# A four-layer graph network on one core: layer 0's second product in Strassen's form, and the order of emission kept on four engines

## The chip, the core and the metric

The kernel runs on one core of one Trainium2 chip. A core has five engines that work at the same time, each from its own queue, in the order of that queue: TensorE (PE: matmuls, with a weight load PEld ahead of each), VectorE (DVE), ScalarE (ACT), GpSimd (POOL) and SyncE (SP, which here only issues DMAs). The metric is device time of one launch in microseconds (us); lower is better. The time before is 2439.52 us, the median of three runs (2439.32 to 2441.19).

## What is computed

Input x holds 128 graphs of 64 nodes with 256 features, in f32, with one 64x64 adjacency matrix for all. Four layers follow one another, each as `x = layernorm(x + layer(x))`. Layer 0 is the one that the change rewrites:

```python
A_norm = A + jnp.eye(n)
A_hat = A_norm * dinv[:, None] * dinv[None, :]
agg = jnp.einsum('nm,bmd->bnd', A_hat, features)
h = jax.nn.relu(_batchnorm(agg.reshape(-1, d) @ W1.T + b1, g1, be1))   # 512 wide
out = _batchnorm(h @ W2.T + b2, g2, be2)                               # 256 wide
```

Both batch norms take mean and variance over all 128 x 64 rows, so nothing behind one can begin before all rows in front of it are done. Layer 1 normalises a Laplacian by the largest eigenvalue of the adjacency matrix (`lam_max = eigvalsh(L)[-1]`), and has a dense layer, attention over the graph and a feed-forward part, with layer norms between. Layer 2 is two graph convolutions and four LSTMs over windows of 1 to 4 nodes, layer 3 one graph attention.

## The kernel before

**Blocks and buffers.** The 8192 rows are cut into 16 blocks of 512 rows. A block is a tile of 128 partitions x 1024 values, either with tokens or with features on the partitions. There are four PSUM tiles (`PS`) and eight SBUF scratch tiles (`mem`); both are handed out and given back by hand.

**Who sets the order.** Each piece of work is a generator. Before it emits instructions it yields `step(engine, us, ps, sl, ...)`: the engine (T is PE, V DVE, S ACT, G POOL, Q a DMA issue), a planned cost, and the PSUM and scratch tiles that it needs. `flow()` (L130) holds a clock for each engine, always lets the step begin that can begin soonest, and so emits the instructions of all generators in one interleaved order. A step that is ready is planned 2.0 us later on PE than it could begin (0.5 us on DVE and ACT in the second flow) unless its stream is `urgent`. There are two flows: one for layer 0 with the eigenvalue, and one for all the rest. After that, the framework's scheduler places the emitted instructions in each engine's queue, and may put a later one ahead of an earlier one. In the built program, counted by emission number, 392 of the 7236 matmuls and transposes on PE stand behind one that is emitted after them, and 1326 of the 2864 instructions on DVE.

**Layer 0.** `first_block` (L523): aggregation with the adjacency (L322, eight products of 128 columns), a copy out of PSUM (DVE L537), two halves of the first dense product (L346, four products of 512 columns each), each followed by two evictions with bias on ACT (L549) and two batch norm statistics on DVE (L553). `bn_coeffs` (L501): aggregates of the statistics (DVE L508), a power on POOL (L511), three small products and sums on DVE (L513 to L515). `second_block` (L556): four relus with the batch norm's scale and shift on ACT (L561), eight products of 512 columns with W2T (PE L566: two halves of output features, four chunks of input features), two evictions (ACT L575), two statistics (DVE L579).

**The eigenvalue**, `eig` (L446): 26 rounds. Each squares a 128x128 matrix M on PE (L468), takes its trace on DVE (L471, L473) and PE (a product with ones, L476), and scales M by one over the trace (DVE L479, L481). Its generator runs in the same stream as the blocks, so its rounds lie between their products. It holds one PSUM tile, `e_ps`, until the flow has ended. From the result it makes `LnT` (L499), the matrix with which layer 1 aggregates.

**From layer 0 to layer 1.** Between the flows the code emits weight loads and a few small instructions. W2 of layer 1 goes to `WB[:, 2:4]` (L609). `wL` and the LSTM biases `bih`, `bhh` (L855 to L872) are loaded into memory that layer 0's pool has given back, and DVE adds the two biases (L873). Then the second flow begins with `end_block` (L631: batch norm on ACT L638, transposes L340, residual sum on DVE L646, layer norm with statistics L272 to L274, the power on POOL L308, the application on ACT L314) and `block` (L652: layer 1; aggregation L322, copy L660, dense product L358, sum L669, a layer norm on DVE with L297 and L300, residual L673, transposes L334, projections L346).

**The LSTMs** (`lstm`, L922) have steps p > 1 in Strassen's form already: seven products of half the rows (L1024) with sums on DVE (L1068, L1070, L1083, L1090, L1092), one on POOL (L1072) and copies on ACT (L1064).

Of the kernel before, what the change touches and what calls it, by code (L numbers as in the profile page):

```python
# [10 lines left out]
AF = mybir.ActivationFunctionType  # L11
ALU = mybir.AluOpType
# [21 lines left out]
def kernel(ctx: ExitStack, tc: tile.TileContext, a: dict, out: bass.AP):  # L34
    nc = tc.nc
    V, S, G, T = nc.vector, nc.scalar, nc.gpsimd, nc.tensor

    def bc_mid(ap, n):

# [10 lines left out]
    def fm(s):  # L50

        return s.rearrange("p (c k) -> p c k", c=2)
# [159 lines left out]
    def ctile(shape, name, pool=cp):  # L212
        return pool.tile(shape, F32, tag=name, name=name)
# [152 lines left out]
    def by_chunk(ap):  # L366
        return ap.rearrange("(k p) m -> p k m", p=P)
# [19 lines left out]
    with c0:  # L387
# [7 lines left out]
        cols = {k: ctile([P, 4 if j < 3 else 2], f"l0{k}", wp) for j, k in enumerate(("b1", "g1", "be1", "b2", "g2", "be2"))}  # L395
        nc.scalar.dma_start(cols["b1"], a["L0_gnn_b1"])
        W2T = ctile([P, 4, D], "W2T", wp)

        def later_loads():
            for k in cols:  # L400
                if k != "b1":
                    yield step("Q", 1.0)
                    nc.sync.dma_start(cols[k], a[f"L0_gnn_{k}"])
            yield step("Q", 6.0)
            nc.sync.dma_start(W2T, by_chunk(a["L0_gnn_W2"]))
            yield step("V", 1.2)
            V.tensor_tensor(adj2, bdA[:, :N], bdA[:, N:], ALU.add)

            V.tensor_scalar(cap1, adj2, 0.0, BIG, ALU.is_gt, ALU.mult)
            V.tensor_scalar(cap1, cap1, -1.0e9, None, ALU.add)  # L410

            V.tensor_scalar(cap3, adj2, 0.0, 2.0, ALU.not_equal, ALU.mult)
            V.tensor_scalar(cap3, cap3, -1.0, BIG, ALU.add, ALU.mult)
# [8 lines left out]
        def etile(name, n=P, bufs=2):  # L422
            return ep.tile([P, n], F32, tag=name, name=name, bufs=bufs)
# [19 lines left out]

        def eig():  # L446
            yield step("V", 1.2)
            V.tensor_scalar(Sy, Sy, 0.5, None, ALU.mult)
# [13 lines left out]
            V.tensor_scalar(sh, sh, 1e-30, None, ALU.add)  # L462
            M = etile("eM")
            V.scalar_tensor_tensor(M, ident, sh, Sy, ALU.mult, ALU.add)
            for _ in range(EIG_STEPS):
                yield step("T", 0.5)
                pm = pse(P)
                T.matmul(pm, M, M, start=True, stop=True)  # L468
                yield step("V", 0.6)
                t_ = etile("etmp")  # L470
                V.tensor_tensor(t_, pm, ident, ALU.mult)  # L471
                d_ = etile("ed", 2)
                V.reduce_sum(d_[:, 0:1], t_, axis=AX.X)  # L473
# [23 lines left out]
            t_ = etile("etmp")  # L497
            V.tensor_scalar(t_, bdAT, 2.0, r_, ALU.mult, ALU.mult)
            V.tensor_tensor(LnT, t_, ident, ALU.subtract)  # L499

        def bn_coeffs(name, nch, st, g, be):  # L501

# [53 lines left out]
        def second_block(i):  # L556
            sc1, sh1 = bn["bn1"]
            src = [(fm(Xs[i]) if f < 2 else H[i])[:, f % 2, :] for f in range(4)]
            yield step("S", 2.8)
            for f in range(4):  # L560
                S.activation(src[f], src[f], AF.Relu, scale=sc1[:, f : f + 1], bias=sh1[:, f : f + 1])  # L561
            yield step("T", 6.9, ps=1)
            ps = PS.take()
            for c in range(2):
                for f in range(4):
                    T.matmul(  # L566
                        fm(PS[ps])[:, c, :],
                        W2T[:, f, c * P : (c + 1) * P],
                        src[f],
                        start=(f == 0),  # L570
                        stop=(f == 3),
                    )
            yield step("S", 1.3, ps=-1)
            for c in range(2):
                S.activation(H[i][:, c, :], fm(PS[ps])[:, c, :], AF.Identity, bias=cols["b2"][:, c : c + 1])  # L575
            PS.give(ps)
            yield step("V", 1.25)
            for c in range(2):
                V.bn_stats(st2[:, c, i, :], H[i][:, c, :])  # L579
            mark("l0b", i)  # L580

        blocks = range(NBLK)
        tasks = [(None, lambda i=i: first_block(i), 2) for i in blocks]
        tasks[1:1] = [(None, eig, 0)]
        tasks[4:4] = [(None, later_loads, 0)]
        tasks.append(
            (
                lambda: ready(*[("l0a", i) for i in blocks]),
# [1 line left out]
                0,  # L590
            )
        )
        tasks += [(lambda: ready(("bn1",)), lambda i=i: second_block(i), 0) for i in blocks]
        tasks.append(
            (
                lambda: ready(*[("l0b", i) for i in blocks]),
# [1 line left out]
                0,  # L598
            )
        )  # L600
        flow([Stream(6, 0, tasks)], {"T": 2.0})
        PS.give(0)


        Wc, Wq, Wk, Wv = (WA[:, j, :].rearrange("p (k m) -> p k m", k=2) for j in range(4))
# [1030 lines left out]
```

## Time and profile before

| | |
|---|---|
| median of 3 runs | 2439.52 us (2439.32 to 2441.19) |
| the profiled execution | 2439.17 us, of which the span from the first to the last instruction is 2437.4 us |
| PE busy | 2348.3 us, 96% of the span, mean granted clock 0.983 |
| DVE, ACT, POOL busy | 1215.1, 1169.9 and 566.7 us (50%, 48%, 23%) |
| DMA | 57.5 MB, 24 GB/s on average |

The profile comes from one execution. Its page has the busy time of each engine, the span in 40 slices, the chain that ended last, and groups of equal instructions with the idle time in front of them and who ended it. "PE L340 <- ACT h L964" reads: PE stood idle ahead of an instruction of line 340, and what released it was the instruction of line 964 on ACT that works on a tile h. A matmul in f32 appears as two records (two passes), a transpose as one. The granted clock is the rate of PE's clock, 1.00 or 0.50 at any one time in this trace; a stage's number is the mean over it.

### The profile page before, as it was taken

The page shows a single profiled execution, that of the slowest core. Times are in us where ns is not written, and L with a number is a line of the kernel's source. Part 1 is how long each engine was busy: PE and PEld are TensorE (multiplying, and loading weights), DVE is VectorE, ACT ScalarE, POOL GpSimd, SP SyncE. Part 2 cuts the span into 40 slices and gives each one's busy share as a digit, 9 for nine tenths or more (in the row PEclk, how much of TensorE's full clock was granted, in tenths as well). Part 3 has the DMA queues.
Part 4 walks back from the last instruction along what each step waited for, and adds up shares of the span by engine and source line. Part 5 has one row for each costly group of instructions (what it writes and reads, how often), then busy time and mean ns, then how long its engine had stood idle before and what let it go on. Part 6 is the DMA issues. An engine that isn't in the chain of part 4 may idle for free. (4 is left out here: it accounts for less than half of the span.)

```text
span 2437.4 us, 33965 instructions
## 1 busy us (share of the span) xinstructions
PE 2348.3 (96%) x13700; PEld 1798.9 (74%) x13700; DVE 1215.1 (50%) x2864; ACT 1169.9 (48%) x2138; POOL 566.7 (23%) x426
## 2 busy tenths in 40 slices
PE   8999889999999999999999999999999999998997
PEld 5544567766676666676676788899999888887785
DVE  4542377646475345744462433344435444455446
ACT  2255453543444444335544444444444654468766
POOL 0000034222333222422231221222212222122112
PEclk9999989999999999999999999999999999999998
DMA  5110111000000000000010000000001000001111
GB/s 172 44 52 0 40 31 49 27 9 10 1 10 18 10 9 10 1 10 34 20 61 1 18 1 1 1 18 1 1 1 35 1 9 10 18 27 66 40 35 44
DMA packets 40974, 57.47 MB, mean 24 GB/s; under 512 B 4592, under 2 KB 33904, under 8 KB 40816
## 3 DMA queue, kind: packets, MB, share of 16 engines
q1 hardware_dynamic: 39712, 54.22, 6.9%
q8 instruction: 107, 1.75, 0.3%
q10 hardware_dynamic: 1104, 1.08, 0.1%
q14 instruction: 51, 0.42, 0.1%
HBM read 38.52 MB, written 16.78 MB: 23 GB/s over the span
## 5 line engine op out<-in xcount | busy, mean ns | idle before, releaser
L1024 PE MATMUL ps<-x,x 128*128 128x256 f32 x1024 | 248.6, 380 | 0.7 <-DVE t L1092 0.7
L1024 PEld LDWEIGHTS ps<-x,x 128*128 128x128 f32 x1024 | 191.5, 190 | 26.4 <-issue 1.6
L314 ACT ACTIVATE x<-x,ln_nm,ln_rs 128x256 f32<-128x256 f32 x196 | 103.7, 592 | 97.0 <-DVE ln_nm L311 95.5
L1024 PE MATMUL ps<-t,x 128*128 128x256 f32 x576 | 141.0, 379 | 0.0
L308 POOL TENSOR_TENSOR ln_rs<-ln_rs,neghalf 128x4 f32<-128x4 f32 (+1 forms) x72 | 70.5, 980 | 231.1 <-DVE ln_rs L274 217.3
L1024 PEld LDWEIGHTS ps<-t,x 128*128 128x128 f32 x576 | 108.6, 190 | 14.6 <-issue 0.4
L346 PE MATMUL ps<-t,W1T 128*128 128x512 f32 x256 | 115.2, 593 | 0.0
L952 PE MATMUL ps<-h,wL 128*128 128x192 f32 (+2 forms) x504 | 111.6, 375 | 0.0
L952 PEld LDWEIGHTS ps<-h,wL 128*128 128x128 f32 x504 | 79.1, 190 | 27.6 <-issue 26.7
L272 DVE BATCH_NORM_STATS2 ln_st<-x 128x6 f32<-128x256 f32 x256 | 98.2, 404 | 0.5
L1100 ACT ACTIVATE t<-t,bih 128x512 f32<-128x512 f32 (+2 forms) x63 | 41.0, 652 | 107.6 <-DVE t L1090 105.9
L952 PE MATMUL ps<-h,x 128*128 128x256 f32 x384 | 86.8, 379 | 0.0
L964 ACT ACTIVATE t<-ps,bih 128x512 f32<-128x512 f32 (+3 forms) x104 | 61.5, 642 | 44.0 <-PE ps L952 43.9
L294 POOL TENSOR_TENSOR ln_rs<-ln_rs,neghalf 128x4 f32<-128x4 f32 x32 | 36.9, 1153 | 188.8 <-DVE ln_rs L274 188.6
L346 PEld LDWEIGHTS ps<-t,W1T 128*128 128x128 f32 x256 | 46.3, 190 | 46.4 <-issue 46.4
L952 PEld LDWEIGHTS ps<-h,x 128*128 128x128 f32 x384 | 72.9, 190 | 10.3 <-issue 0.5
L1083 DVE COPY t<-ps 128x256 f32<-128x256 f32 (+2 forms) x63 | 23.7, 378 | 113.5 <-PE ps L1024 113.5
L273 DVE BATCH_NORM_AGGREGATE ln_mv<-ln_st 128x2 f32<-128x6 f32 x448 | 71.3, 167 | 0.0
L346 PE MATMUL ps<-t,wA 128*128 128x512 f32 x144 | 67.9, 617 | 2.8 <-ACT t L681 2.8
L952 PE MATMUL ps<-t,wL 128*128 128x512 f32 x144 | 64.9, 607 | 2.5 <-ACT t L1250 2.5
L1090 DVE TENSOR_TENSOR t<-ps,t 128x512 f32<-128x512 f32 (+2 forms) x63 | 38.1, 604 | 54.8 <-PE ps L1024 47.9
L1100 ACT ACTIVATE x<-x,bih 128x512 f32<-128x512 f32 (+2 forms) x57 | 36.6, 641 | 55.7 <-DVE x L1090 55.4
(692 smaller groups left out, 5688.2 us busy)
## 6 DMA issues: line engine op xcount, KB each, us to landing
t<-in_x_dram SPq DMA_DIRECT2D x26, 512.0 KB, 3.9
xd<-x SPq DMA_DIRECT2D x16, 512.0 KB, 2.6
x<-xd SPq DMA_DIRECT2D x6, 512.0 KB, 3.3
out_dram<-x SPq DMA_DIRECT2D x6, 512.0 KB, 3.0
wL<-in_L_gnn_Wih_dram SPq DMA_DIRECT2D x2, 1024.0 KB, 4.9
h<-in_x_dram SPq DMA_DIRECT2D x4, 512.0 KB, 4.2
x<-in_L_gnn_Whh_dram SPq DMA_DIRECT2D x2, 1024.0 KB, 4.9
t<-xd SPq DMA_DIRECT2D x4, 512.0 KB, 3.3
```

Of the source, the lines that this page charges most:

```text
L272: V.bn_stats(st[:, t, :], y[:, t, :])
L273: V.bn_aggr(mv[:, t, :], st[:, t, :])
L294: G.tensor_tensor(rs, rs, neghalf[:, :NT], ALU.pow)
L308: G.tensor_tensor(rs, rs, neghalf[:, :n], ALU.pow)
L314: S.activation(y[:, t, :], y[:, t, :], AF.Identity, scale=rs[:, t : t + 1], bias=nm[:, t : t + 1])
L346: T.matmul(ps[:, c, :], w[:, k, (off + c) * P : (off + c + 1) * P], yT[:, k, :], start=(k == 0), stop=(k == nk - 1),)
L952: T.matmul(spread(fm(PS[ps])[:, j, :n], q), WL[p][0][:, k, m], x_of(0, q)[:, k], start=(k == 0), stop=(k == 1),)
L964: S.activation(of(sl)[:, j], fm(PS[ps])[:, j, :n], AF.Tanh if g == 2 else AF.Sigmoid, bias=bias(g, c))
L1024: T.matmul(dst, WS[p][name](k, g), y[:, k], start=first and k == 0, stop=k == 1, skip_group_check=not first)
L1083: V.tensor_copy(y[:, 1, :], v[:, 0, :])
L1090: V.tensor_tensor(y[:, 0:2, :], v[:, 2:4, :], y[:, 0:2, :], ALU.add)
L1100: S.activation(of(act[g])[:, 0], of(act[g])[:, 0], f, bias=bias(g, 0))
```

## The change

One: `manual_schedule` keeps the order of emission on PE, DVE, ACT and POOL. The order of SP's DMAs stays with the scheduler.

Two: `second_block` of block 0 runs by chunks (relu of chunk f, then both products with it); blocks 1 to 15 use Strassen's form, with rows split in halves u and v and features in halves x (chunks 0, 1) and h (chunks 2, 3). Seven products of 256 columns, each over two chunks, take the place of eight of 512. Four sums of weights are made once (into the place of layer 1's W2), and each block takes two of the scratch tiles for T1 to T4.

Three: in `eig` only every third round takes the trace and scales; the other squares are copied out of PSUM as they are (26 squares as before, 8 traces in place of 26). It moves to a stream of its own, ahead of the blocks and urgent, and gives its PSUM tile back when it is done.

Four: `later_loads` moves from fifth to fourth place in the tasks.

```diff
+    ctx.enter_context(tc.manual_schedule(engines={E.PE, E.DVE, E.Activation, E.Pool}))
...
+        W2S = WB[:, 2:4, :].rearrange("p a (b k m) -> p (a b) k m", b=2, k=2)
...
+            yield step("V", 1.7)
+            (a11, a21), (a12, a22) = ([W2T[:, k : k + 2, c * P : (c + 1) * P] for c in range(2)] for k in (0, 2))
+            V.tensor_tensor(W2S[0], a21, a22, ALU.add)
+            V.tensor_tensor(W2S[1], W2S[0], a11, ALU.subtract)
+            V.tensor_tensor(W2S[2], a11, a21, ALU.subtract)
+            V.tensor_tensor(W2S[3], a12, W2S[1], ALU.subtract)
...
-            for _ in range(EIG_STEPS):
+            for j in range(EIG_STEPS):
...
+                if j % 3 < 2:
+                    yield step("V", 0.35)
+                    M = etile("eM")
+                    V.tensor_copy(M, pm)
+                    continue
...
+            if i == 0:
+                for f in range(4):
+                    yield step("S", 0.7)
+                    relu(f)
+                    yield step("T", 1.75, ps=int(f == 0), waits=f == 3)
...
+            x, h = fm(Xs[i]), H[i]
+            u, v = slice(0, TB // 2), slice(TB // 2, TB)
+            yield step("V", 1.4, sl=2)
...
+            V.tensor_tensor(T1, x[:, :, v], x[:, :, u], ALU.subtract)
+            V.tensor_tensor(T2, h[:, :, v], T1, ALU.subtract)
+            yield step("G", 1.3, waits=False)
+            G.tensor_tensor(T4, h[:, :, u], T2, ALU.subtract)
+            yield step("V", 0.7)
+            V.tensor_tensor(T3, h[:, :, v], x[:, :, v], ALU.subtract)
...
+            product(A11, x[:, :, u], p[:, 0, :], first=True)
+            product(W2S[0], T1, p[:, 3, :], first=True)
+            yield step("S", 0.75, waits=False)
+            S.copy(y[:, 0, :], p[:, 0, :])
+            S.copy(y[:, 3, :], p[:, 3, :])
+            t = yield step("T", 1.75)
+            product(A12, h[:, :, u], p[:, 2, :])
+            product(W2S[3], h[:, :, v], p[:, 3, :])
+            yield step("T", 0.88)
+            product(W2S[1], T2, p[:, 0, :])
+            yield step("V", 0.42)
+            V.tensor_copy(y[:, 1, :], p[:, 0, :])
+            yield step("T", 0.88)
+            product(W2S[2], T3, p[:, 0, :])
+            yield step("V", 1.1)
+            V.tensor_tensor(y[:, 3, :], p[:, 0, :], y[:, 3, :], ALU.add)
+            V.tensor_tensor(y[:, 0:2, :], p[:, 2:4, :], y[:, 0:2, :], ALU.add)
+            yield step("T", 0.88)
+            product(A22, T4, p[:, 0, :])
...
+            yield step("S", 1.5, ps=-1)
+            S.activation(h[:, 0, :], fm(Xs[i])[:, 0, :], AF.Identity, bias=cols["b2"][:, 0:1])
+            S.activation(h[:, 1, v], y[:, 3, :], AF.Identity, bias=cols["b2"][:, 1:2])
+            S.activation(h[:, 1, u], p[:, 0, :], AF.Identity, bias=cols["b2"][:, 1:2])
...
-        tasks[1:1] = [(None, eig, 0)]
-        tasks[4:4] = [(None, later_loads, 0)]
+        tasks[3:3] = [(None, later_loads, 0)]
...
-        tasks += [(lambda: ready(("bn1",)), lambda i=i: second_block(i), 0) for i in blocks]
+        tasks += [(lambda: ready(("bn1",)), lambda i=i: second_block(i), 2) for i in blocks]
...
-        flow([Stream(6, 0, tasks)], {"T": 2.0})
-        PS.give(0)
+        flow([Stream(1, 0, [(None, eig, 0)], urgent=True), Stream(6, 1, tasks)], {"T": 2.0})
```

More of the change, by code (lines that the diff above doesn't have):

```diff
@@ L36 @@
     V, S, G, T = nc.vector, nc.scalar, nc.gpsimd, nc.tensor
+    E = mybir.EngineType
+    ctx.enter_context(tc.manual_schedule(engines={E.PE, E.DVE, E.Activation, E.Pool}))
     def bc_mid(ap, n):
@@ L397 @@
         W2T = ctile([P, 4, D], "W2T", wp)
+        W2S = WB[:, 2:4, :].rearrange("p a (b k m) -> p (a b) k m", b=2, k=2)
+        W2S = [W2S[:, j] for j in range(4)]
         def later_loads():
@@ L499, in eig @@
             V.tensor_tensor(LnT, t_, ident, ALU.subtract)
+            PS.give(0)
         def bn_coeffs(name, nch, st, g, be):
@@ L558, in second_block, with relu @@
             src = [(fm(Xs[i]) if f < 2 else H[i])[:, f % 2, :] for f in range(4)]
+            def relu(f):
+                S.activation(src[f], src[f], AF.Relu, scale=sc1[:, f : f + 1], bias=sh1[:, f : f + 1])
+            if i == 0:
[3 more added lines that the diff above has]
+                    yield step("T", 1.75, ps=int(f == 0), waits=f == 3)
+                    if f == 0:
+                        ps = PS.take()
+                    for c in range(2):
+                        T.matmul(
+                            fm(PS[ps])[:, c, :],
+                            W2T[:, f, c * P : (c + 1) * P],
+                            src[f],
+                            start=(f == 0),
+                            stop=(f == 3),
+                        )
+                yield step("S", 1.3, ps=-1)
+                for c in range(2):
+                    S.activation(H[i][:, c, :], fm(PS[ps])[:, c, :], AF.Identity, bias=cols["b2"][:, c : c + 1])
+                PS.give(ps)
+                yield from second_stats(i)
+                return
@@ L559, in second_block @@
             yield step("S", 2.8)
             for f in range(4):
-                S.activation(src[f], src[f], AF.Relu, scale=sc1[:, f : f + 1], bias=sh1[:, f : f + 1])
-            yield step("T", 6.9, ps=1)
-            ps = PS.take()
[L564 to L572, printed above, removed]
@@ L573, in second_block @@
-            yield step("S", 1.3, ps=-1)
-            for c in range(2):
-                S.activation(H[i][:, c, :], fm(PS[ps])[:, c, :], AF.Identity, bias=cols["b2"][:, c : c + 1])
+                relu(f)
+            x, h = fm(Xs[i]), H[i]
+            u, v = slice(0, TB // 2), slice(TB // 2, TB)
+            yield step("V", 1.4, sl=2)
+            slots = [mem.take() for _ in range(2)]
+            T1, T2, T3, T4 = (
+                mem[sl][:, j * TB : (j + 1) * TB].rearrange("p (c k) -> p c k", c=2) for sl in slots for j in range(2)
+            )
@@ new lines, in second_block, with product @@
+            V.tensor_tensor(T1, x[:, :, v], x[:, :, u], ALU.subtract)
[4 more added lines that the diff above has]
+            V.tensor_tensor(T3, h[:, :, v], x[:, :, v], ALU.subtract)
+            def product(w, y, dst, first=False):
+                for k in range(2):
+                    T.matmul(
+                        dst, w[:, k, :], y[:, k, :], start=first and k == 0, stop=k == 1, skip_group_check=not first
+                    )
@@ new lines, in second_block @@
+            A11, A12, A22 = (W2T[:, k : k + 2, c * P : (c + 1) * P] for k, c in ((0, 0), (2, 0), (2, 1)))
+            yield step("T", 1.75, ps=1)
+            ps = PS.take()
+            p, y = (m.rearrange("p (j k) -> p j k", j=4) for m in (PS[ps], Xs[i]))
+            product(A11, x[:, :, u], p[:, 0, :], first=True)
[3 more added lines that the diff above has]
+            S.copy(y[:, 3, :], p[:, 3, :])
@@ L576, in second_block @@
+            yield step("T", 0.88)
+            product(A22, T4, p[:, 0, :])
+            for sl in slots:
+                mem.give(sl)
+            yield step("S", 1.5, ps=-1)
+            S.activation(h[:, 0, :], fm(Xs[i])[:, 0, :], AF.Identity, bias=cols["b2"][:, 0:1])
+            S.activation(h[:, 1, v], y[:, 3, :], AF.Identity, bias=cols["b2"][:, 1:2])
+            S.activation(h[:, 1, u], p[:, 0, :], AF.Identity, bias=cols["b2"][:, 1:2])
             PS.give(ps)
+            yield from second_stats(i)
@@ L577, in second_block, with second_stats @@
+        def second_stats(i):
             yield step("V", 1.25)
```

## The prediction, made before the changed kernel ran

> **What bounds the kernel now.** I read the table of stages first: for each stretch its length, then the busy time of PE, PEld, DVE, ACT and POOL with the number of records, then PE's granted clock.
>
> ```profile
> 0.00:155.00 155.00, 147.83 (x578) 86.32 (x578) 78.69 (x160) 40.49 (x63) 2.50 (x15) 1.00 0.36 105
> 155.00:161.00 6.00, 1.94 (x10) 1.37 (x8) 4.12 (x14) 2.24 (x4) 1.01 (x1) 0.72 0.00 1
> 161.00:277.00 116.00, 115.60 (x291) 53.28 (x290) 28.60 (x66) 63.31 (x94) 0.00 (x0) 0.98 0.00 0
> 277.00:283.00 6.00, 1.33 (x5) 0.98 (x5) 4.84 (x20) 2.05 (x4) 0.70 (x1) 0.80 0.01 1
> 283.00:337.00 54.00, 39.48 (x288) 30.07 (x287) 41.27 (x126) 42.09 (x66) 19.23 (x17) 0.85 0.25 74
> 337.00:2180.00 1843.00, 1816.57 (x11096) 1443.54 (x11097) 919.70 (x1978) 826.09 (x1458) 491.97 (x326) 0.99 0.04 13
> 2180.00:2438.00 258.00, 225.55 (x1441) 183.39 (x1439) 137.91 (x505) 193.59 (x454) 51.31 (x66) 0.95 0.15 50
> ```
>
> PE is full in layer 0's products (rows 1 and 3) and nearly full from 337 to 2180: there only PE work that disappears, or a hole in PE, moves the end. The two batch norms (155, 277) and the start of layer 1 (283 to 337) are chains with PE waiting. Behind 337 PE stands idle 1843 - 1816.6 = 26 us, and 32 us behind 2180. A hole costs twice: the granted clock is below 1.00 after it.
>
> Second, the rows of ACT and PE around the largest hole behind 337 (start, length, engine, line, what, [idle before <- who ended it]):
>
> ```profile
> 516.92 1.09 ACT L314 ACTIVATE x<-x,ln_nm,ln_rs 128x256 f32<-128x256 f32 x2 [4.30 <-DVE ln_nm L311]
> 517.92 0.61 ACT L991 ACTIVATE t<-h 128x512 f32<-128x512 f32 x1
> 518.44 1.08 ACT L314 ACTIVATE x<-x,ln_nm,ln_rs 128x256 f32<-128x256 f32 x2
> 519.42 1.24 ACT L964 ACTIVATE h<-ps,bih 128x512 f32<-128x512 f32 x2
> ```
> ```profile
> 520.72 0.69 PE L340 MATMUL ps<-ident,h 128*128 128x128 f32 x2 [3.37 <-ACT h L964]
> ```
>
> PE waits 3.4 us for a PSUM tile that ACT (L964) has not emptied, since ACT stands before a layer norm (L314) that waits for DVE. By emission number L964 (2888) comes ahead of L314 (2932): the scheduler turned them round. The hole at 580 (3.5 us, also "ACT h L964") has the same form: L964 (3236) stands behind L991 (3258), which waits for POOL.
>
> **The change, part by part.** PE's order hardly moves (392 of 7236 out of emission order before); DVE's (1326 of 2864) and ACT's do.
>
> Strassen. In the last rows of the stage ACT empties one block's PSUM every 7.09 us:
>
> ```profile
> 269.38 1.26 ACT L575 ACTIVATE h<-ps,l0b 128x512 f32<-128x512 f32 x2 [5.83 <-PE ps L566]
> 276.47 1.26 ACT L575 ACTIVATE h<-ps,l0b 128x512 f32<-128x512 f32 x2 [5.83 <-PE ps L566]
> ```
>
> In between lie 16 records of L566, whose weight loads follow at 0.4285 us (13 steps from 262.69 to 268.26), so 6.86 us, and one of eig's products, so 0.23 us. Fourteen products of 256 columns are 28 records; the LSTMs' stretch 1400 to 1420 has 94 such in 20.0 us, 0.2128 each, so 5.96 us. 15 blocks x 0.90 = **-13.5**. Beside it, per block: on ACT four relus at 0.70 from start to start and five further instructions (L1064 0.37 twice, L575 0.68, L1104 0.45 twice), 5.1 us; on DVE three sums (L1070, 0.68), a copy and two sums (0.42, 0.41, 0.68) and two statistics (0.68 each), 4.9 us; on POOL one difference, 1.26 (L1044). All below 5.96, so PE stays the bound, but DVE and POOL meet:
>
> ```profile
> 316.14 2.36 POOL L719 TENSOR_TENSOR t<-t,rows 128x1024 f32<-128x1024 f32 x1
> 316.28 2.24 DVE L274 TENSOR_SCALAR ln_rs<-ln_mv 128x4 f32<-128x4 f32 x1
> ```
>
> A DVE instruction of 0.16 us elsewhere lasts as long as the POOL one beside it. If all of T4 delays DVE, DVE needs 4.9 + 1.26 = 6.2 us (5.6 when the 0.08 by which its instructions overlap are taken off): at PE's own rate. Least 0, most 0.9 x 15 = 13.5 (the whole saving); I take **+2**, near the lower end, because dependent products of a block stand four products (3.4 us) apart on PE in the new program.
>
> [...]
>
> Eig: 18 products with ones fewer x 0.23 = **-4.1**; the squares stay. Its DVE work shrinks (0.29 + 0.29 + 0.17 + 0.35 becomes one copy in 18 of 26 rounds), beside a full PE, so nothing. The first-flow order puts one eig product and a wait for three DVE rows (some 0.7) ahead of the first aggregation, while DVE no longer runs the five small rows of L407 to L413 (0.8) in front: **+0.3** (0 to 1). The weight sums are four rows of DVE, half idle there.
>
> First batch norm: before, two of the four aggregates (L508, 1.01 the pair) ran early, at 153.35; kept order puts all four behind the last statistics: **+1.0**. Chunks for block 0: before, its products already follow each relu (160.95, 163.22, 164.71), so 0.
>
> Second batch norm: eig is done, so its rows no longer stand between (-1.1: PE's wait from 276.6 to 282.6 becomes about 4.9). But in block 15 the last product waits for an eviction, block 14's two statistics (1.28) and a sum, +1.6. Net **+0.5**. Sum for layer 0: -13.5 + 2 - 4.1 + 0.3 + 1.0 + 0.5 = **-14** (-19 to 0).
>
> Start of layer 1. Kept order puts the sum of the LSTM biases (L873) ahead of block 0's residual sum (L646) on DVE. Its data come late:
>
> ```profile
> 283.56 0.37 SPq L855 DMA_DIRECT2D wL<-in_L_gnn_Wih_dram  x1
> ...
> 286.84 0.45 SPq L381 DMA_DIRECT2D bhh<-in_L_gnn_bhh_dram  x1
> ```
> ```profile
> 294.71 0.18 DVE L873 TENSOR_TENSOR bih<-bih,bhh 128x32 f32<-128x32 f32 x1
> ```
>
> wL waits for layer 0's pool; bhh follows 3.28 us behind it and lands 4.7 us later (the tile's own view). In the new program that queue can go on when the batch norm is done, some 4 us after the last product, so L646 begins at about 12.1 + 0.2 us behind it; before, 285.05 - 276.3 = 8.7. So **+3.7** where there was cover. Against it: block 0's statistics (286.31 to 290.97, mixed with other blocks' sums) run in one piece, -2.2; its dense product, mixed with others from 297.1 to 303.0, too, -2.5; but ACT takes block 1's layer norm ahead of block 0's copy, +2.3, and DVE another block's statistics, +2.8: block 0 reaches its transposes (L334, 313.65) 4 us late. Block 1, next at 333.42, gains the same 4 from whole steps. **0** (-6 to +8). SP also holds layer 1's W2 until the last Strassen product; its first use is at 418, so that is hidden.
>
> 337 to 2180. The holes at 517 and 580 go: PE's idle time there is 3.8 (516 to 530) and 3.5 (580 to 600), and the granted clock 0.76 and 0.83 loses 0.24 x 14 and 0.17 x 20, 3.4 each: **-14**. The other holes (19 idle, and 5 of clock at 980 and 1100) I take as replaced by equal ones, as kept order has waits of its own. Least: all 38 go. Most: the slower rival, +29.
>
> Tail, 2180 on: **0** (-12 to +12, a quarter of its 32 idle and some 14 of clock).
>
> **Sum**: -14 + 0 - 14 + 0 = -28 on the profiled execution's 2439.17 (2437.4 span and 1.8 around it) = 2411.2. The median shown is 0.35 higher: **2411.5**.
>
> **Rivals.**
> A, more holes go: two thirds of the other 24 behind 337 and 12 of the tail, -28 more: 2383.5. For it: the two largest both come from turned order. Against: PE's order was kept all along. Chance 0.22.
> B, kept order is neutral, as every hole has a substitute: only layer 0's -14, 2425.5. Chance 0.15.
> C, the change doesn't do what it says: DVE, held by POOL, becomes the bound of the Strassen stage, +0.9 a block, and order is neutral: 2439. For it the 6.2 against 5.96; against it POOL is idle there apart from T4. Chance 0.08.
> D, slower: DVE stands before a layer norm's second half (L300, L311) until POOL's power is done. The wait is in the trace (0.90 and 1.12 us). In kept order nothing passes it: 80 norms in layer 1 x 1.1 = 88 us of DVE. If one wait in three holds a PSUM tile that PE needs, +29: 2439.5 - 14 + 29 = 2454.5. It decides from 14 of 88, one in six. Against it: the code yields another step between the power and its use. Chance 0.10.
> The forecast itself (2400 to 2424) has 0.45.
>
> So faster 0.82 (forecast, A, B), within 0.2% (4.9 us, about what a measurement of this kernel tells from no change) 0.08, slower 0.10. The range 2380 to 2440 leaves out D and the better half of A.
>
> **What would show it.** In the new profile: 15 blocks of the stage behind the first batch norm at about 6.0 us each on a PE that is over 97% busy (C: below 90%, DVE near full); no "L340 <- ACT h L964" above 1 us; block 0's residual sum released by a DMA or standing right behind the bias sum, some 12 us after the last Strassen product; four aggregates in a row. I am wrong if DVE waits on POOL's power before PE's holes (D), or if the stretch behind layer 1's start is longer than before.

## The result and the profile after

The changed kernel takes **2464.56 us** (2463.35 to 2466.24, four runs) against 2439.42 for the kernel before beside it: ratio **1.0102** (95% interval 1.0084 to 1.0119). It is slower by 1.0%; the forecast was 2411.5. The profiled execution has a span of 2462.5 us, 25.1 more than before.

First the same table of stages as for the kernel before (length, then busy time of PE, PEld, DVE, ACT and POOL with records, PE's granted clock, DMA share and rate). The ends of the stages are those of the same instructions, as near as a whole row allows, and the long stretch from 337 to 2180 is cut where the first Strassen product of an LSTM begins, first in the kernel after:

```profile
0.00:163.40 163.40, 152.58 (x586) 89.03 (x586) 77.01 (x161) 40.48 (x63) 2.50 (x15) 1.00 0.27 77
163.40:170.10 6.70, 0.02 (x1) 0.02 (x1) 3.77 (x10) 2.15 (x4) 1.01 (x1) 0.76 0.00 0
170.10:278.00 107.90, 101.61 (x436) 82.34 (x436) 68.55 (x121) 76.85 (x140) 20.07 (x15) 0.98 0.08 24
278.00:282.60 4.60, 0.05 (x1) 0.05 (x1) 3.06 (x10) 1.34 (x3) 1.16 (x5) 0.66 0.07 25
282.60:342.00 59.40, 41.75 (x291) 31.64 (x292) 41.85 (x108) 27.51 (x42) 10.64 (x9) 0.77 0.26 78
342.00:1290.60 948.60, 931.95 (x6332) 652.93 (x6331) 611.99 (x1226) 430.56 (x561) 299.15 (x182) 0.99 0.05 19
1290.60:2206.00 915.40, 883.46 (x4755) 787.89 (x4754) 392.37 (x771) 401.39 (x918) 201.02 (x147) 1.00 0.02 8
2206.00:2462.50 256.50, 224.58 (x1448) 185.30 (x1447) 148.32 (x501) 188.74 (x451) 51.08 (x67) 0.94 0.15 50
```

and then the two parts of that stretch in the kernel before:

```profile
337.00:1299.70 962.70, 941.25 (x6334) 657.98 (x6335) 535.64 (x1213) 416.60 (x538) 292.69 (x179) 0.99 0.05 18
1299.70:2180.00 880.30, 875.32 (x4763) 785.56 (x4762) 384.06 (x765) 409.50 (x920) 199.28 (x147) 1.00 0.03 8
```

Read the lengths first. Stage by stage the change takes and gives: the first dense products became 8 us longer (163.4 for 155), the stage with Strassen's form 8 shorter (107.9 for 116), the start of layer 1 5 longer (59.4 for 54), layer 1's body 14 shorter (948.6 for 962.7). All of that and more is lost in the LSTMs: 915.4 for 880.3, with nearly the same count of matmuls (4755 and 4763 records). Of that stretch PE stands idle 915.4 - 883.5 = 32 us, where before it was 880.3 - 875.3 = 5. The change never touched a line there; only the order of the instructions differs.

For the comparison of many kernels I use five stages cut by single instructions: *layer 0* to the first transpose of layer 1's start, *start* to block 0's transposes to features (L334 before, L336 after), *layer 1* to the first Strassen product of an LSTM (L1024, L1105), *LSTM* to the last such product, *tail* to the end. All are us of the profiled execution; the time is the median, with its ratio to the kernel before as it ran beside each (2439.4 to 2440.7).

| kernel | layer 0 | start | layer 1 | LSTM | tail | time | ratio (95%) |
|---|---|---|---|---|---|---|---|
| before | 282.6 | 31.0 | 986.1 | 925.5 | 212.1 | 2439.42 | |
| after | 282.5 | 36.5 | 971.6 | 969.3 | 202.5 | 2464.56 | 1.0102 (1.0084 to 1.0119) |
| order_alone | 284.9 | 38.2 | 971.7 | 969.6 | 202.6 | 2469.01 | 1.0117 (1.0102 to 1.0132) |
| work_alone | 272.7 | 30.2 | 987.1 | 925.6 | 211.9 | 2429.53 | 0.9950 (0.9933 to 0.9966) |
| kept_to_lstm | 283.2 | 36.6 | 980.6 | 926.8 | 209.9 | 2438.55 | 0.9992 (0.9982 to 1.0001) |
| act_free | 281.2 | 37.1 | 984.5 | 965.7 | 207.1 | 2479.28 | 1.0159 (1.0144 to 1.0174) |
| dve_free | 276.6 | 30.0 | 965.2 | 960.3 | 204.1 | 2438.86 | 0.9988 (0.9979 to 0.9997) |
| pe_free | 272.2 | 36.6 | 972.7 | 934.9 | 206.3 | 2424.85 | 0.9937 (0.9923 to 0.9950) |
| kept_layer1 | 273.8 | 33.3 | 970.4 | 928.7 | 209.8 | 2419.06 | 0.9911 (0.9897 to 0.9924) |
| strassen_alone | 277.2 | 30.6 | 988.9 | 925.5 | 211.8 | 2436.63 | 0.9984 (0.9975 to 0.9993) |
| pe_kept_lstm | 273.4 | 30.5 | 984.1 | 958.0 | 206.8 | 2451.31 | 1.0049 (1.0034 to 1.0064) |
| bias_later | 282.2 | 31.4 | 972.6 | 969.4 | 202.5 | 2459.82 | 1.0086 (1.0071 to 1.0101) |
| copies_dve | 271.8 | 29.8 | 988.7 | 925.7 | 211.7 | 2428.62 | 0.9957 (0.9942 to 0.9972) |
| layer1_dve_free | 273.5 | 31.3 | 964.7 | 929.9 | 209.5 | 2411.57 | 0.9885 (0.9869 to 0.9902) |
| plan_lag | 273.8 | 38.7 | 889.6 | 1092.3 | 216.5 | 2513.66 | 1.0305 (1.0286 to 1.0323) |
| both | 272.2 | 30.1 | 964.0 | 930.1 | 212.2 | 2409.93 | 0.9876 (0.9861 to 0.9892) |

(For plan_lag the border between layer 1 and LSTM means little: in its order the first Strassen product comes before layer 1 has ended.)

The chain that ends last, which is mostly one long PE chain in both kernels, would not have shown this; the lengths of equal stages did.

### The profile page after: what moved, and what is told of

Read it like the earlier page. It is cut to its first block, busy times and chain, and to the rows that moved or that the text cites. A ratio compares the mean times of both kernels' runs of the same rounds, so it can differ in the third digit from the quotient of the medians.

```text
span 2462.5 us, 34476 instructions
## 1 busy us (share of the span) xinstructions
PE 2336.0 (95%) x13844; PEld 1829.2 (74%) x13844; DVE 1346.9 (55%) x2904; ACT 1169.0 (47%) x2179; POOL 586.6 (24%) x441
## 5 line engine op out<-in xcount | busy, mean ns | idle before, releaser
L1105 PE MATMUL ps<-x,x 128*128 128x256 f32 x1024 | 248.3, 380 | 1.9 <-DVE x L1173 1.1
L1105 PEld LDWEIGHTS ps<-x,x 128*128 128x128 f32 x1024 | 191.7, 190 | 28.5 <-DVE x L1173 1.9
L316 ACT ACTIVATE x<-x,ln_nm,ln_rs 128x256 f32<-128x256 f32 x196 | 102.0, 592 | 82.8 <-DVE ln_nm L313 82.7
L1105 PE MATMUL ps<-t,x 128*128 128x256 f32 x576 | 140.2, 379 | 0.6 <-DVE h L1173 0.3
L1105 PEld LDWEIGHTS ps<-t,x 128*128 128x128 f32 x576 | 108.7, 190 | 15.4 <-issue 0.7
L275 DVE BATCH_NORM_AGGREGATE ln_mv<-ln_st 128x2 f32<-128x6 f32 x448 | 81.5, 182 | 15.3
L1045 ACT ACTIVATE x<-ps,bih 128x512 f32<-128x512 f32 (+3 forms) x80 | 47.3, 642 | 71.7 <-PE ps L1033 71.6
L1171 DVE TENSOR_TENSOR t<-ps,t 128x512 f32<-128x512 f32 (+2 forms) x63 | 38.2, 606 | 72.0 <-PE ps L1105 65.5
L1143 ACT COPY t<-ps 128x256 f32<-128x256 f32 (+2 forms) x63 | 21.3, 338 | 104.2 <-PE ps L1105 100.6
L1164 DVE COPY x<-ps 128x256 f32<-128x256 f32 (+2 forms) x57 | 21.2, 371 | 80.4 <-PE ps L1105 80.1
```

What stands on the lines that cost most here:

```text
L275: V.bn_aggr(mv[:, t, :], st[:, t, :])
L316: S.activation(y[:, t, :], y[:, t, :], AF.Identity, scale=rs[:, t : t + 1], bias=nm[:, t : t + 1])
L1045: S.activation(of(sl)[:, j], fm(PS[ps])[:, j, :n], AF.Tanh if g == 2 else AF.Sigmoid, bias=bias(g, c))
L1105: T.matmul(dst, WS[p][name](k, g), y[:, k], start=first and k == 0, stop=k == 1, skip_group_check=not first)
L1164: V.tensor_copy(y[:, 1, :], v[:, 0, :])
L1171: V.tensor_tensor(y[:, 0:2, :], v[:, 2:4, :], y[:, 0:2, :], ALU.add)
```

## The experiments

### Is it the order or the new work? order_alone, work_alone

The first is the kernel before with one line added, the second the changed kernel without it:

```diff
+    ctx.enter_context(tc.manual_schedule(engines={E.PE, E.DVE, E.Activation, E.Pool}))
```

> The kernel before with the order of emission kept on PE, DVE, ACT and POOL, and no other edit. Theory (the kept order itself makes the LSTMs slow, whatever layer 0 does): the stretch of the Strassen LSTMs (first to last product of L1024) about 44 us longer, as in the changed kernel, the stretch between the first LSTM product and layer 1's last product some 14 shorter, the tail some 10 shorter; about 2460 in all. Rival (the new layer 0 shifts the phase of the later work and the LSTMs meet by accident): the LSTM stretch stays within 10 of before, 2415 to 2440.

> The changed kernel without the kept order: Strassen form, first block by chunks and the new eigenvalue stay, the scheduler orders the queues. Theory: the LSTM stretch as before (925 us, not 969), layer 0 shorter by some 5 to 14, so 2425 to 2434. Rival (the loss comes with the new work): 2450 or more.

Measured: 2469.0 with the order alone, 2429.5 with the new work alone. The LSTM stretch is 969.6 in the first and 925.6 in the second, as long as in the kernel after and in the kernel before. Layer 1 is 14 shorter in both kernels that keep the order on all four engines from end to end (971.6 and 971.7). So each part of the order's effect is there without the new layer 0, and the rival (a shifted phase) is out. The new work is worth 9.9 us of the span, all of it in layer 0.

### Can the stages be had apart? kept_to_lstm

```diff
+    kept = ctx.enter_context(ExitStack())
+    kept.enter_context(tc.manual_schedule(engines={E.PE, E.DVE, E.Activation, E.Pool}))
...
-            units.append((lambda p=p, need=need: ready(("w", p), *need), lambda u=u: unit(*u[1:]), 7))
+            units.append((lambda p=p, need=need: ready(("w", p), *need), lambda u=u: (kept.close(), unit(*u[1:]))[1], 7))
```

> The changed kernel, but the order is kept only until the first LSTM unit over windows of two begins to be emitted; from there the scheduler orders. Theory: layer 1 keeps its gain of some 9 to 14 and the LSTMs do not lose 44: 2464.6 - 44 + 10 (the tail's gain given back) = about 2430, between 2415 and 2435. Rival (what was kept ahead of the LSTMs sets their phase): above 2450.

Measured 2438.6, above the 2415 to 2435 of the theory. The LSTMs lose next to nothing now (926.8), as the theory says, but layer 1 is 9 longer than with the order kept throughout. Two rows of PE from the switch (start, length, what, [idle before <- who ended it]) show why for most of it:

```profile
1275.43 6.15 PE L348 MATMUL ps<-x,Wg 128*128 128x512 f32 x8 [4.06 <-ACT x L1313]
...
1296.96 3.60 PE L348 MATMUL ps<-x,Wg 128*128 128x512 f32 x8
```

At the switch the scheduler put a layer norm that waits for DVE (L316, four instructions) and three more ACT instructions ahead of a copy (L1313) that had been emitted before them all; with the order kept, that copy runs first. PE waited 4.06 us, and then eight products took 6.15 us that take 3.60 a little later: the granted clock is 0.58 over those 6 us. A single hole of 4 us cost 6.6.

### Which engine's order? act_free, dve_free, pe_free

The same line, each time with one engine left out:

```diff
-    ctx.enter_context(tc.manual_schedule(engines={E.PE, E.DVE, E.Activation, E.Pool}))
+    ctx.enter_context(tc.manual_schedule(engines={E.PE, E.DVE, E.Pool}))
```

> The changed kernel with the order kept on PE, DVE and POOL, ACT left to the scheduler. Theory (ACT stands before a copy whose product is not there yet, and the gate activation that empties a PSUM tile waits behind it): most of the 44 us of the LSTM stretch goes, 2425 to 2440. Rival (DVE's final sums L1171 and L1173, kept behind other DVE work, are what holds PSUM): the stretch keeps more than 30 of the 44, 2455 to 2465.

> The changed kernel with the order kept on PE, ACT and POOL, DVE left to the scheduler. ACT's kept order was not the cause (ACT left free: the LSTM stretch still 965.7 us against 969.4). Theory now: DVE, in order, stands at a sum or copy whose product is not there yet while a sum that is ready, and that a PSUM tile waits for, is queued behind it; then the LSTM stretch falls from 969 to 925-935 and the time to 2425-2440. Rival (PE's own kept order: PE stands before a product whose operand is late, while another unit's product could run): the stretch stays above 950, time 2450-2470.

> The changed kernel with the order kept on DVE, ACT and POOL, PE left to the scheduler (160 of its 7308 instructions then stand behind a later one). Theory (DVE): PE's order was nearly that of emission before too, so the LSTM stretch stays within 10 of 969 and the time at 2455-2470. Rival (PE): the stretch falls to 925-940, the time to 2420-2440.

Measured: 2479.3, 2438.9 and 2424.9. My theory had been ACT, because the trace of the kernel after has PE waiting for ACT's L1185 most often in that stretch. It fell: with ACT free the LSTMs still take 965.7. DVE, my second theory, fell as well: 960.3 (the time, 2438.9, lies in the theory's range, but by layer 0, the start and layer 1, not by the LSTMs). With **PE** free they take 934.9. Only 160 of PE's 7308 instructions then stand ahead of one that was emitted earlier, and these give back 34 of the 44 us. (My expectation for pe_free words this count the wrong way round.)

How so few can do so much is seen in PE's rows. In the kernel after, around one of attention's small blocks (L1531 transposes, ACT copies the result out of PSUM in L1533, L1541 is the product):

```profile
2000.01 1.13 PE L1105 MATMUL ps<-x,x 128*128 128x256 f32 x4 [0.25 <-DVE t L1173]
2001.70 0.68 PE L1531 MATMUL ps<-ident,x 64*64 64x64 f32 x16 [0.56 <-ACT t L1185]
2002.86 0.68 PE L1531 MATMUL ps<-ident,x 64*64 64x64 f32 x16 [0.47 <-ACT x L1533]
2004.01 1.09 PE L1541 MATMUL ps<-t,x 64*64 64x256 f32 x16 [0.47 <-ACT x L1533]
2006.58 2.07 PE L1105 MATMUL ps<-h,wB 128*128 128x256 f32 x4 [1.48 <-DVE x L1552]
```

and the same instructions with PE left to the scheduler:

```profile
1980.94 0.68 PE L1531 MATMUL ps<-ident,x 64*64 64x64 f32 x16
1981.55 1.13 PE L1105 MATMUL ps<-x,x 128*128 128x256 f32 x4
1982.62 0.68 PE L1531 MATMUL ps<-ident,x 64*64 64x64 f32 x16
1983.23 0.70 PE L1105 MATMUL ps<-x,x 128*128 128x256 f32 x2
1983.86 1.09 PE L1541 MATMUL ps<-t,x 64*64 64x256 f32 x16
1986.43 1.13 PE L1105 MATMUL ps<-h,wB 128*128 128x256 f32 x4 [1.48 <-DVE x L1552]
```

In the first, each of attention's groups waits for ACT, which works on the result of the group in front of it (0.56, 0.47 and 0.47 us), and a product ahead of them waits 0.25 for DVE. In the second, LSTM products (L1105) stand between, and these four waits, 1.75 us in all, are gone; the wait of 1.48 behind L1541 stays. The products were there in the first kernel too, but behind. The half clock goes as well: behind the wait of 1.48 the first kernel's four products take 2.07 us, at a granted clock of 0.50 from 2006.62 to 2010.03, and the second's 1.13, at 1.00.

The three runs say more of layer 1. With ACT free, nearly all of its gain is gone (984.5): at 525 PE waits 5.5 us for the eviction that was L964 in the kernel before, and at 416 another 6.4 for ACT. With DVE free, layer 1 is 965.2, shorter than with all four kept. PE's order does not matter there (972.7).

### PE's order alone: pe_kept_lstm

Everything is left to the scheduler until the first LSTM unit over windows of three; from there the order is kept on PE and on nothing else:

```diff
+    def late():
+        if not kept_on:
+            kept_on.append(kept.enter_context(tc.manual_schedule(engines={E.PE})))
...
+            ... lambda u=u: (late(), unit(*u[1:]))[1] if u[1] == 3 else unit(*u[1:]), 7))
```

> The changed kernel with everything left to the scheduler, but from the first LSTM unit over windows of three on the order is kept on PE alone. Theory (with PE in order, products that could run stand behind one whose operand is late; freeing PE alone took the LSTM stretch from 969.4 to 934.9 us, freeing DVE or ACT alone only to 960.3 and 965.7): the stretch grows from 925.5 by 20 to 40, time 2445 to 2470 against 2429.5 of the run with no order kept. Rival (it takes PE, DVE and ACT in order together; PE alone does little): the stretch stays below 935, time 2430 to 2438.

Measured 2451.3, and 958.0 for the LSTMs against 925.6: PE's kept order is enough for 32 of the 44 us (the execution profiled is the slowest of the four, 3.3 us above the median, so perhaps 29). The rival, that it takes several engines together, is out for these. The other 11 were not taken apart: some 3 may lie ahead of that unit (kept_layer1, which keeps all four up to it, has 928.7), the rest goes with the order of the other three engines (pe_free still has 934.9). Where the 44 show, in whole stretches, first of the kernel after, then of work_alone, in the columns of the table of stages:

```profile
1290.60:2260.00 969.40, 931.05 (x5098) 829.60 (x5097) 426.83 (x876) 440.88 (x1017) 210.26 (x157) 0.99 0.03 11
```
```profile
1290.03:2215.58 925.55, 916.09 (x5065) 820.97 (x5063) 413.70 (x858) 448.03 (x1002) 207.77 (x155) 1.00 0.03 11
```

Idle time of PE is 969.4 - 931.1 = 38.3 against 9.5: 29 of the 44. The other 15 are busy time: 33 records more that moved here from the tail (33 x 0.2161, some 7, which the tail has less) and the clock, 0.99 for 1.00.

### The start of layer 1: bias_later

```diff
-    V.tensor_tensor(bl, bl, bh, ALU.add)
...
     def gcn_rows():
+        V.tensor_tensor(bl, bl, bh, ALU.add)
```

> The changed kernel, order kept on all four engines, with the sum of the LSTM biases emitted behind the begin of block 3 in place of ahead of block 0. Theory (the prediction's step: this sum waits for the DMA of bhh until 290.08 and block 0's residual sum stands behind it until 290.19, though PE's transposes for it end by 284): the residual sum starts at 284 to 286, block 0's transposes to features come 4 to 5 us earlier against the last product of layer 0, time 2464.6 - 4 = about 2460. Rival (the layer norm chains behind it are as late anyway, as block 1 waits for the same engines): within 2 of 2464.6.

In the kernel after, DVE's rows are:

```profile
290.08 0.19 DVE L954 TENSOR_TENSOR bih<-bih,bhh 128x32 f32<-128x32 f32 x1 [7.77 <-DMA bhh<-in_L_gnn_bhh_dram]
290.19 1.22 DVE L727 TENSOR_TENSOR x<-ps,t 128x1024 f32<-128x1024 f32 x1
```

DVE stands 7.77 us before the small sum, and block 0's residual sum (L727) follows right behind, 12.3 us after the last product of layer 0 (277.9). With the sum moved, the start takes 31.4 in place of 36.5 and the whole 2459.8 in place of 2464.6: 4.7 of the 5 us at the start arrive at the end, so the rival is out.

### Layer 0: strassen_alone, copies_dve

strassen_alone is the new second product with the old eigenvalue in its old stream and no kept order. copies_dve is the changed kernel without kept order and with this edit:

```diff
-            yield step("S", 0.75, waits=False)
-            S.copy(y[:, 0, :], p[:, 0, :])
-            S.copy(y[:, 3, :], p[:, 3, :])
+            yield step("V", 0.75, waits=False)
+            V.tensor_copy(y[:, 0, :], p[:, 0, :])
+            V.tensor_copy(y[:, 3, :], p[:, 3, :])
```

> The kernel before with the second product in Strassen's form (and block 0 by chunks, the sums of weights, the two scratch tiles), the old eigenvalue in its old stream and no kept order. By the prediction's terms: 2440 - 13.5 + 2 = 2428.5. Theory after the runs so far (without kept order layer 0 is 9.9 shorter in all, of which the eigenvalue's 18 fewer products with ones should be 4): Strassen's form gives only some 6, about 2434, because PE waits for evictions and sums at the blocks' turns. Rival (Strassen gives its 11 to 13 and the eigenvalue as it is now put costs): 2427 to 2430, that is less than or equal to the run with both.

> The changed kernel without kept order, with the two copies of a Strassen block (the ones that ACT does while its queue is full of relus: ACT busy 40.00 of 40 us at the beginning of the stage) on DVE. Theory (ACT bounds the first blocks of the Strassen stage: 28 products take 9.48 in place of 6.04 us): the first 28 products take 1 to 3 us less, the stage 1.5 to 3 less than 104.0; time 2427 to 2428. Rival (the first blocks wait for their sums on DVE or for PE's slow clock behind the batch norm): the stage stays at 104 or grows, as DVE gets 0.75 us a block more; time 2429 or more.

strassen_alone: 2436.6, layer 0 shorter by 5.4. With the new eigenvalue as well (work_alone) it is 9.9, so that one, fewer products and a stream of its own together, is worth 4.5. The steady blocks are as forecast; all of these are PE's records of L623 in the kernel after:

```profile
240.00:260.00 20.00, 20.00 (x94) 17.62 (x93) 1.00 0.10 26
```

94 records in 20 us, as many as the forecast counted in the LSTMs; but that counts the two that the window cuts as well. From start to start they are 0.216 apart, 28 of them 6.04. What is missing lies around the steady part. One piece of it nobody had in view (DVE in work_alone):

```profile
15.45 0.43 DVE L413 TENSOR_TENSOR wB<-W2T 128x256 f32<-128x256 f32 x1 [2.22 <-DMA W2T<-in_L_gnn_W_dram]
```

Left to itself, the scheduler puts the first sum of weights ahead of the copy of an aggregated block, where it waits for W2T's transfer, and PE waits 1.8 us at 15.8 (2.4 in strassen_alone). In the kernel after, with the order kept, the sums come behind the copies, at 18.27, and cost nothing. This was read from the rows; the sums alone were not moved.

copies_dve: 2428.6 against 2429.5, the stage 102.9 against 104.0. The gain is smaller than expected, within the scatter of the times, and not where I expected it: the first 28 products still take 9.48. They do so because eight of block 0's records lie between them (8 x 0.4285 = 3.43, 9.48 - 3.43 = 6.05); that ACT was full there was no cause. What went is mostly farther on: the block of 6.82 takes 6.04, that of 6.40 takes 6.20.

### The stages put together: kept_layer1, layer1_dve_free, both

The order is kept only from block 0 of layer 1 to the first LSTM unit over windows of three. kept_layer1 keeps it on all four engines; layer1_dve_free leaves out DVE; both is layer1_dve_free with the copies on DVE. The edit of layer1_dve_free:

```diff
-        seq.append((lambda i=i: ready(("end", i)), lambda i=i: block(i), 5))
+        seq.append((lambda i=i: ready(("end", i)), lambda i=i: (kept.enter_context(tc.manual_schedule(engines={E.PE, E.Activation, E.Pool})) if i == 0 else None, block(i))[1], 5))
...
+            ... lambda u=u, p=p: (kept.close() if p == 3 else None, unit(*u[1:]))[1], 7))
```

> The changed kernel with the order kept only from block 0 of layer 1 to the first LSTM unit over windows of three; layer 0, the start of layer 1 and the later LSTMs are left to the scheduler. Theory (gains and losses of the order belong to stages and can be had apart): the run without kept order, 2429.5, less the 14 that layer 1 gains from the order: 2412 to 2420. Rival (the stages' gains are a matter of phase and are given back at the switch, as the 4.06 us hole in front of L348 and its products at half the clock, 6.15 in place of 3.60, did when the order was kept to the first unit over windows of two): 2425 or more.

> The changed kernel with the order kept on PE, ACT and POOL (not on DVE) from block 0 of layer 1 to the first LSTM unit over windows of three, and all else left to the scheduler. From the runs by stage: layer 0 272.75 (no order), layer 1 with DVE left free 995.2 (as against 1003.7 with all four kept), LSTMs 928.7 and tail 209.7 (as with the order kept in layer 1 alone): 2406 of span, 2409 in all. Rival (stage gains do not add up, since the phase at the switch decides): 2415 or more.

> The run layer1_dve_free (order kept on PE, ACT and POOL in layer 1 alone) with the two copies of a Strassen block on DVE. Theory (terms of different stages add up): 2411.6 less the 1.1 that the copies took from the stage (102.9 in place of 104.0): about 2410.5, not to be told from 2411.6 by more than the scatter. Rival (the shift at the start of layer 1 changes what follows): 2415 or more.

Measured: 2419.1, 2411.6 and **2409.9** (ratio 0.9876, 0.9861 to 0.9892). Theory holds over rival in all three. The stages nearly add up: the times lie 3.6, 2.6 and 0.6 us from the sums made beforehand from other runs' stages (2415.5, 2409 and 2410.5). The last one is faster than both kernels, by some 30 and 55 us; that it is faster than layer1_dve_free is within the scatter.

### Is the plan too tight? plan_lag

```diff
-LAG, LAG_T = 0.06, 0.2
+LAG, LAG_T = 0.3, 0.6
```

> The changed kernel, order kept on all four engines, with the planner's latencies raised from 0.06 and 0.2 (behind PE) to 0.3 and 0.6 us; the work is the same, the emitted order differs. Theory (the plan hands PE products whose operands it believes to be there and that come some tenths of a us late): the LSTM stretch falls by 15 or more from 969, time 2435 to 2450. Rival (where two units are all that is there, any kept order has late operands, and only an order that adapts to the real rows helps): the stretch stays within 10 of 969, time 2455 to 2475.

Measured 2513.7, the slowest of all: theory and rival both fell. Longer latencies in the plan make another order, with holes of its own (PE waits 11.3 us for ACT at 278, 5.8 for ACT at 1163 and 8.7 for POOL at 1213), while layer 0 comes out at 273.8, 8.7 better than with the old latencies. So a kept order is as good as the plan happens to be, stage by stage; why this plan is bad in the LSTMs was not settled.

## Why the prediction was wrong, by its own steps

Its terms for the kernel after, beside what the runs show in the five stages:

| step | forecast | measured |
|---|---|---|
| layer 0 | -14 | -0.1 (-9.9 without kept order) |
| start of layer 1 | 0 | +5.5 |
| layer 1 | -14 | -14.5 |
| LSTMs ("replaced by equal ones") | 0 | +43.8 |
| tail | 0 | -9.6 (some 7 of it records moved into the LSTMs) |
| sum | -28 | +25.1 |

**The step that failed** is "The other holes ... I take as replaced by equal ones, as kept order has waits of its own", with what stood ahead of it: "PE's order hardly moves". I took the few matmuls that the scheduler had moved as a sign that PE's order is of no weight. In its place the runs show that PE's kept order alone costs 32 us in the LSTMs (pe_kept_lstm) and that freeing PE alone gives back 34 (pe_free). In the rows at 2000 the moved products fill the time that would else be idle; that all of them do was not followed up one by one. (In layer 1 the same step failed the other way, see below.) Behind 1300 PE had 5 us idle in 880, and I looked for what the order could still take away there, not for what it had already taken. Their number said nothing of their worth: 160 of 7308 are worth 34 us in the LSTMs.

**Layer 1** came out at the forecast's number, but in the main by luck. Counted from block 0's transposes to features, PE has 6510 records there in each of these kernels, and at every border below the same instructions, by line, lie ahead of it. Lengths by stretch, in us:

| records | what lies there before | before | after | act_free | dve_free |
|---|---|---|---|---|---|
| 0 to 300 | block 1 of the start | 37.4 | 33.1 | 32.1 | 32.4 |
| 300 to 1000 | | 90.7 | 96.4 | 99.5 | 92.8 |
| 1000 to 1500 | the hole at 517 | 80.3 | 76.1 | 82.4 | 76.1 |
| 1500 to 1900 | the hole at 580 | 73.9 | 72.0 | 71.0 | 65.5 |
| 1900 to 4500 | | 381.0 | 383.5 | 385.6 | 382.1 |
| 4500 to the end | holes at 991, 1014, 1099 | 322.9 | 310.5 | 313.9 | 316.4 |

The two holes that were to give 14 gave 4.2 and 1.9 (the kernel after has two of its own close behind, 2.58 us at 529 and 2.43 at 587). A new one, with PE waiting 3.56 us for DVE at 422, took 5.7, and at record 4500 the kernel after is 3.3 us later than the kernel before (980.1 against 976.9). The gain comes behind that: 12.4 us, where these holes of the kernel before are gone or smaller (1.47 is left of the first):

```profile
990.99 1.97 PE L334 MATMUL ps<-ident,x 128*128 128x128 f32 x8 [3.42 <-DVE t L1222]
...
1014.48 5.77 PE L952 MATMUL ps<-t,wL 128*128 128x512 f32 x9 [2.53 <-ACT t L1250]
...
1098.63 3.58 PE L346 MATMUL ps<-x,wA 128*128 128x512 f32 x5 [2.35 <-ACT x L681]
```

They belong to "the other holes" that the prediction took as replaced by equal ones. It is the kept order that took them (order_alone has 310.5 there, work_alone 322.9), but not ACT's: with ACT free 9.0 of the 12.4 remain. Which engine's order it was is open.

At 517 the reason given is right: with ACT free a hole of 5.5 us that ends with the same eviction is back. At 580 it is not shown: with ACT free that stretch is no longer than with all four kept (71.0 and 72.0). At the old place of the first hole the kernel after has:

```profile
527.35 2.08 ACT L316 ACTIVATE x<-x,ln_nm,ln_rs 128x256 f32<-128x256 f32 x4 [2.15 <-DVE ln_nm L313]
...
529.38 1.98 PE L348 MATMUL ps<-t,wB 128*128 128x512 f32 x4 [2.58 <-DVE x L727]
```

ACT still waits for the layer norm, but PE no longer waits for what is behind it on ACT; the wait that is late next is DVE's residual sum. That one goes with DVE's kept order: with DVE free it is gone too, and layer 1 is another 6.4 shorter.

**Layer 0: Strassen's form.** The rate was nearly right (6.04 us a block for the forecast 5.96), and in the steady blocks PE stays the bound; rival C, DVE held by POOL, did not come (DVE is busy 30.2 of 40 us from 210 to 250 in work_alone, PE 39.5). Over the whole stage of the kernel after PE is busy 101.6 of 107.9 us, 94%, below the 97% that the prediction named as its sign. The steady blocks lose 15 x 0.08 = 1.2 against the forecast, by the count of records above. That DVE and POOL hold each other up is seen in a few rows: in work_alone the sum L615 at 218.31 takes 1.68 us beside POOL's T4 (218.16 to 219.43), and about 0.7 in the others. In the kernel after, T4 takes 1.59 to 1.60 us in the three rows that begin beside a sum L619 (173.70, 177.23, 180.75) and 1.27 to 1.28 in the other twelve, and L619 takes 0.85 to 0.88 in the three rows that begin while T4 runs (209.80, 235.45, 261.13) and 0.68 to 0.69 in the others. But most of T4 falls beside statistics and sums out of PSUM, which keep their length (in the kernel after 1.27 to 1.28 for a pair of L662 and 0.68 for L647, with T4 beside them and without). What reached PE is at most the 0.8 us of the one block behind the row at 218.31, the 6.82 below. (The prediction took 2 us for T4's cost to PE, and 13.5 at most; the rows show at most those 0.8.) The stage itself, without kept order, is 104.0 for 115.4 - 4.0 (the eigenvalue's share), a gain of 7.4 where 13.5 - 2 was written (the share: 18 and 17 records before, two a product, 0.23 each). Missing from 13.5 are the steady 1.2, the last block's two waits (0.58 and 1.44, of which 1.6 was booked at the batch norm), 1.6 in blocks of 6.08 to 6.82, and about 1.3 that is left over, at block 0 and its slow clock (0.55 from 164.1 to 169.0 in work_alone) as far as is known. With the order kept, PE stands three more times before h's products until ACT has made a copy (L635) that lies behind relus: 2.06, 1.10 and 1.10 us, and the stage is 107.8.

**Layer 0: the eigenvalue.** The new one gave 4.5 us where it could (forecast 4.1). In kept order it did not. "Beside a full PE, so nothing" was wrong: each round stands on PE at its planned place, and when DVE's part is late, the queue behind it waits. In the list of waits of the first 164 us of the kernel after (who waited for whom: total, times, longest) these are:

```profile
PE ps L480 <- DVE eM L498: 1.6, 3, 0.5
PE ps L467 <- DVE ed L464: 1.3, 1, 1.3
PE ps L493 <- DVE ed L490: 1.2, 2, 0.6
```

PE is idle 5.3 us between its first product and the last W1T product, where before it was 0.5, and that product ends 8.3 later. Some of it is work moved from the second stage: all 26 squares lie here now, 16 before. With PE free, the same stage has 0.4 idle and ends 2.7 later than before, so that much is the moved work. With the order kept but the old eigenvalue (order_alone) it has 0.4 idle as well: it is the new rounds in kept order that cost. The two batch norms were sized right: 6.72 in place of 5.91 for the first (+0.8 for +1.0), 4.64 in place of 6.27 for the second, behind waits of 1.9 us in the last block.

**Start of layer 1.** Mechanism and moment were right: the residual sum behind the bias sum, 12.3 us after the last product. Block 0 reaches its transposes 5.4 late (forecast 4), and so does block 1, 5.0 late (338.45 for 333.42). The offset, "Block 1 ... gains the same 4 from whole steps", came some 18 us later than written: 4.3 us in the first 300 records of the table above, which my stages count to layer 1. There the kernel after is 1.0 us behind the kernel before (352.1 for 351.1), so the term comes out near its 0, and layer 1 behind it at -10.2. It was no reason to leave the wait in: bias_later has it out, and the end is 4.7 earlier.

**Rival D** had the sign, and with 2454.5 a time 10 short of the result, but not the place. It put the loss on DVE in layer 1's norms; layer 1 gained. Its wait is there once, in the hole at 422: DVE stands 1.12 us for POOL's power, then takes the norm's next step (2.29), and the sum that PE waits for (L824) stands behind both. With DVE free PE waits 1.59 there in place of 3.56. It was the right kind of wait (what is ready stands behind what is not) on an engine that I had put aside because it is the busiest.

## What to carry to other kernels

When an order is taken from a scheduler, ask of the bottleneck engine first what the few moved instructions were moved for: an instruction that stands out of order may be the filling of a hole, and its worth is then the hole, not its share of the count. Keep the order stage by stage, on the engines where a run shows a gain, and leave the rest alone: the same switch was worth -14 us in one stage and +44 in another. When a stage comes out at the number forecast, cut it further at equal work: here less than half of layer 1's 14 lay at the holes that were to give it. A wait that is put down to one engine (here ACT, by the list of waits) can have its remedy on another, namely on the one that waits and has other work.

## What the runs showed of the hardware

In the kernel after, PE's clock fell to half behind holes of 1.48, 1.90 and 2.43 us, but not behind one of 2.58. Three windows of the kernel after, each beginning where a hole ends:

```profile
529.38:531.50 2.12, 2.12 (x5) 1.06 (x6) 2.12 (x3) 2.10 (x4) 0.99 (x1) 1.00 0.57 230
```
```profile
586.60:588.50 1.90, 1.90 (x9) 1.90 (x10) 1.71 (x2) 0.00 (x0) 0.00 (x0) 0.52 0.00 0
```
```profile
2204.56:2207.00 2.44, 2.44 (x10) 2.44 (x11) 2.27 (x10) 0.12 (x1) 0.00 (x0) 0.51 0.00 0
```

Behind the hole of 2.58 us at 529 the clock is 1.00; behind one of 2.43 at 587 it is 0.52, and behind one of 1.90 at 2204 it is 0.51. Behind one of 1.48 us, with shorter ones just ahead of it (0.25 to 0.56), it is 0.50 in the kernel after (2006); without these it is 1.00 in pe_free (1986, where the four products take 1.13 us in place of 2.07). In these rows the length of the hole alone does not decide; what else does was not shown. So the prediction's "A hole costs twice" holds for some of these holes and not for others.

Behind the holes that end at 587, 787, 2007, 2174 and 2205 the clock is 0.50 for 3.4 us each time (2204.59 to 2208.00, for one) and then 1.00, so each costs 1.7 us beside its own length: 1.90 becomes 3.6. By these five, a hole of 2 us in this kernel is to be priced at up to 3.7, nearly twice its length; that is an estimate.
